# Four graph attention layers on one core: the order in which the lists of sources are made

## The chip, the cores and the metric

The kernel runs on one core of one Trainium2 chip. The metric is the device time of one execution in microseconds (us). The engines are named as in the profile: PE (TensorE, matrix products), DVE (VectorE), ACT (ScalarE), POOL (GpSimd) and SP (SyncE, which only issues transfers here).

## The reference

Four layers of graph attention over the same graph of 4096 nodes, with 256 features each. Every layer normalises `x`, projects it, weighs the sources of each target by a softmax over its neighbours and adds the result to `x`. The layers differ in their weights, in heads (1, 1, 4, 1 with a positive and a negative attention) and in the last function. Layer 0, cut to what matters:

```python
h = jnp.maximum(_layernorm(x, axis=-1), 0.0) @ W.T + b_W
e = (h @ a1)[:, None] + (h @ a2)[None, :] + b_a[0]
e = jnp.where(e > 0, e, 0.2 * e)
scores = jnp.where(adj > 0, e, -9e15)
x = x + jax.nn.softmax(scores, axis=1) @ h
```

The graph is sparse and uneven: an entry of `adj` is 1 with a probability proportional to `((1 + i) * (1 + j)) ** -0.5`, so the first nodes have many neighbours and the last ones few.

## The kernel before

The 4096 targets are 32 tiles of 128, and 4 tiles make a block of 512 (blocks 0 to 7). Sources come in the same 32 tiles; the first four of them (`DP`) are always taken whole.

**Dense and listed.** In layer 0, blocks 0 to 3 (tiles 0 to 15) are computed dense: for each of the 32 source tiles DVE makes weights of 128 x 512 (L1154) and PE multiplies them with the features in four products of 128 x 257 (L1196). This is a dense step. Blocks 4 to 7 (tiles 16 to 31) are computed from lists: for each target tile only the sources that one of its targets reads are gathered, by indirect DMAs. A listed tile has 4 steps with the first source tiles, then 1 to 5 steps with gathered rows `s_gg`, then 1 or 2 steps ("quads", `s_gq`, L1110, L1133) in which each quarter of 32 targets has rows of its own. `DENSE = (4, 2, 1, 1)`: in layer 1 only blocks 0 and 1 are dense, in layers 2 and 3 only block 0. So the lists of blocks 4 to 7 are read by all layers, those of blocks 2 and 3 from layer 1 on, and that of block 1 from layer 2 on.

**Masks.** `mask_chunk` turns the integer matrix (`s_raw`, loaded by SP, L1449) into bytes (`s_m`, L1468), stores them and notes in `seen` which sources have any edge (L1475). The masks of dense blocks are made as those blocks are computed; those of blocks 4 to 7 are made on the side, one chunk every three dense steps (`sides`). The last chunk of a block (`c == NCH - 1`) starts its list. In dense steps counted from 0, this happens at step 23 for block 4, 47 for 5, 60 for 1, 71 for 6, 92 for 2, 95 for 7 and 124 for 3.

**Lists.** `list_sources(ib, ...)` makes the lists of the four tiles of a block. It is a generator of some fifty small pieces: DVE operations on 128 x 112 or 128 x 448 (L886 to L935), prefix sums on PE (`pre`, `tot`, L868 and L870, twice), and then for each of the four tiles 28 small matmuls (`idx_ps`, L971) with one-hot matrices that DVE makes (`first`, L946), and the copy to `idx_T` (L981). Its temporary tiles exist once, so two lists overlap little.

**The gathers.** `gather` (L529) issues one indirect DMA of 128 rows from POOL, with a pause (a memset, L538) after every second one. POOL's instructions run in the order in which the program issues them. For a tile there are gathers of mask bytes (`mlist`) and of features (`s_gg`, `s_gq`), and both need `idx_T`.

**Order of the work.** `run` goes over a plan of steps, with fetch, begin, weigh and multiply 0, 2, 3 and 6 steps apart (`LEAD`). After each step it adds the step's cost to a clock of its own and takes two pieces of the first generator of the queue `lists_q`, if that is due (a piece can ask for a delay of up to 4 units). The queue is first in, first out. When a step fetches a tile whose list is not there, `listed_sources` takes pieces at once until it is:

```python
while T not in index:
    pump(lists_q, 1, force=True)
```

Listed steps of layer 0 are mixed with dense steps from dense step 48 on (`LISTED0`), one or two after each. At the end of layer 0's plan the rest of `lists_q` is taken by force; layer 1's plan comes after it. On PE, DVE, ACT and SP a scheduler sets the final order from this order of issue; POOL's order is kept.

Of the kernel before, what the change touches and what calls it, by code (L numbers as in the profile page):

```python
# [480 lines left out]
TW = tuple(FRONT[l] + GW[l] + MW * ((l, True) in MASKS_IN.values()) for l in range(4))  # L481
LEAD = (0, 2, 3, 6)
RUN = 2


@with_exitstack
def list_layers(ctx: ExitStack, tc: tile.TileContext, a: dict, out: bass.AP, flag):
# [39 lines left out]
    def gather(dst, src, index_ap, offset):  # L527
# [8 lines left out]
        gathers[0] += 1  # L536
        if gathers[0] % RUN == 0:
            nc.gpsimd.memset(pause, 0.0)  # L538
# [22 lines left out]
    def mask_rows(b, jt):  # L561
        if b not in MASKS_IN:
            return table_rows(mask_t[b], jt)
        l, behind = MASKS_IN[b]
        c0 = FRONT[l] + GW[l] if behind else 0
        return table_rows(table[l], jt)[:, :, c0 : c0 + MW].bitcast(U8)
# [116 lines left out]
    posts, lists_q = [], []  # L683
    clock = [0.0]

    def push(queue, work, delay=0.0):
        queue.append([work, clock[0] + delay])
# [703 lines left out]
    with ExitStack() as phase:  # L1391
        prep = phase.enter_context(tc.tile_pool(name="s_prep", bufs=1))
        lists_p = phase.enter_context(tc.tile_pool(name="s_lists", bufs=1))
# [41 lines left out]
            order += [(DENSE[0] + k // NCH, k % NCH) for k, at in enumerate(sides) if at == s]  # L1435
        loaded = {}
        seen = {}

        def load():

            n = len(loaded)
            if n == len(order):
                return
            ib, c = order[n]
            loaded[order[n]] = []
            for h in range(2):
                raw = stage.tile([P, half, IB], I32, name=f"s_raw_{ib}_{c}_{h}", tag="raw")
                r0 = (c * CH + h * half) * P
                nc.sync.dma_start(  # L1449
                    raw,  # L1450
                    a["adjT"][r0 : r0 + half * P, ib * IB : (ib + 1) * IB].rearrange(
                        "(c p) i -> p c i", p=P
                    ),
                )
                loaded[ib, c].append(raw)

        def mask_chunk(ib, c):

            load()
            if ib == 0:  # L1460
                behind(c)
            m = (
                mpre[:, :, ib * IB : (ib + 1) * IB]
                if c == 0
                else mpool.tile([P, CH, IB], U8, name=f"s_m_{ib}_{c}", tag="m")
            )
            for h, raw in enumerate(loaded[ib, c]):
                nc.vector.tensor_scalar(m[:, h * half : (h + 1) * half, :], raw, 0.0, None, op0=ALU.is_gt)  # L1468
            if c > 0 or ib in MASKS_IN:
                nc.sync.dma_start(mask_rows(ib, c * CH), m)  # L1470
            if ib > 0:
                if c == 0:
                    seen[ib] = lists_p.tile([P, IT * GR, JT], BF16, name=f"seen_{ib}", tag="seen", bufs=4)
                else:
                    nc.vector.tensor_reduce(  # L1475
                        seen[ib][:, :, (c - 1) * CH : c * CH].rearrange("p a j -> p j a"),
                        m.rearrange("p j i -> p (j i)")
                        .bitcast(I32)
                        .rearrange("p (j a w) -> p j a w", j=CH, w=GP // 4),
                        AX.X,  # L1480
                        ALU.max,
                    )
                if c == NCH - 1:
                    push(lists_q, list_sources(ib, seen[ib], lists_p, consts))
            return m

        def behind(c):

            if c + 4 < NIB:
                load_x(c + 4)  # L1490
            if c == 4:
                zero_rows()
            if c == 5:
                L1 = weights(1, const, prep, nc.sync)
                L1.pre = keep.tile([P, DP, GW[1]], F32, name="pre1")
                L1.rows = rows_of(L1, rows)
                L1.pool = rows
                next(L1.making)
                push(posts, L1.making, 15.0)

        def block(ib):
            masks = {}

            def get(jt):
                if jt % CH == 0:
                    masks[jt // CH] = mask_chunk(ib, jt // CH)
                for k, at in enumerate(sides):
                    if at == ib * NT + jt:
                        mask_chunk(DENSE[0] + k // NCH, k % NCH)
                ensure(lambda: L0.ready[jt])  # L1510
                return [0], [L0.g[:, jt, :]], masks[jt // CH][:, jt % CH, :]

            return Unit(L0, ib * IT, IT, NT, get, big="growb", rates=(2, 2, 1))
# [5 lines left out]
        consts = list_constants(lists_p)  # L1519
# [130 lines left out]
def gat_layers(tc: tile.TileContext, a: dict, out: bass.AP):  # L1650
    nc = tc.nc
    with tc.tile_pool(name="flag", bufs=1) as pool:
        flag = pool.tile([1, 1], I32, name="flag")

        with tc.manual_schedule(engines={mybir.EngineType.Pool}):
            list_layers(tc, a, out, flag)
        again = nc.values_load(flag[0:1, 0:1], min_val=0, max_val=1)
        with tc.If(again > 0):
            dense_layers(tc, a, out)
# [45 lines left out]
```

## Time and profile before

| | |
|---|---|
| median of 3 runs | 1554.24 us (1552.2 to 1558.08) |
| profiled execution | 1687.46 us, span 1685.7 us |
| mean granted TensorE clock in it | 0.923 |
| PE, PE weight loads | 1452.5 us (86%), 1091.1 us (65%) |
| DVE, ACT, POOL | 1176.8 us (70%), 494.3 us (29%), 1066.3 us (63%) |
| layer 0, from the span's start | to about 561 us |

The profiled execution is longer than the median of the runs and ran at a lower TensorE clock. Busy time is time in which an engine executes; the idle time before an instruction is shown with what released it. For a POOL gather the busy time is that of issuing it. Lines L... are those of the kernel before.

### The profile page before, as it was taken

The numbers are of one execution on the slowest core, as the hardware profiler recorded it, in microseconds if no ns is written. First come the engines' busy times: TensorE is split into PE (matmuls) and PEld (weight loads), VectorE is DVE, ScalarE is ACT, GpSimd is POOL, SyncE is SP. The second block draws the span as 40 slices with busy tenths as digits, with TensorE's granted clock in tenths as the row PEclk, the third lists the DMA queues.
The fourth block names the chain that finished last, engine by engine and source line by source line (L and its number), as shares of the span: only waits on it lengthen the run. The fifth ranks groups of instructions, "written<-read, shape, count | busy, mean of one in ns | idle before, by whom it ended". The sixth has DMA issues, their size and how long they took to land.

```text
span 1685.7 us, 30113 instructions
## 1 busy us (share of the span) xinstructions
PE 1452.5 (86%) x10558; PEld 1091.1 (65%) x10558; DVE 1176.8 (70%) x3383; ACT 494.3 (29%) x1558; POOL 1066.3 (63%) x1292
## 2 busy tenths in 40 slices
PE   6999899768648989988798889898877989899995
PEld 4887677557536867766545555556655767677773
DVE  6888989857727456855498889787754455577754
ACT  5631021002001112423334555466744111111111
POOL 9816888582381467757607678665665266777775
PEclk9999999979778899999999999998977999999997
DMA  7899877745322445545513344333343366767665
GB/s 264 291 325 294 280 239 248 246 125 134 87 49 87 124 118 141 146 134 146 154 51 111 92 110 110 93 108 88 104 116 100 116 181 191 220 186 216 199 183 148
DMA packets 150091, 267.82 MB, mean 159 GB/s; under 512 B 21824, under 2 KB 74637, under 8 KB 149933
## 3 DMA queue, kind: packets, MB, share of 16 engines
q0 software_dynamic: 43440, 123.46, 27.1%
q1 hardware_dynamic: 105656, 141.83, 26.2%
q8 instruction: 86, 1.41, 0.3%
q14 instruction: 73, 0.59, 0.1%
q10 hardware_dynamic: 836, 0.53, 0.1%
HBM read 224.84 MB, written 40.90 MB: 158 GB/s over the span
## 4 chain that ended last, share of the span: by engine, by line
PE 62%; DVE 16%; issue 6%; another core or an unknown queue 5%; DMA 4%; POOL 3%; ACT 2%; SPq 0%; POOLq 0%; DVEq 0%; ACTq 0%
PE s_acc L1196 36%; PE s_pj L774 8%; DVE s_p L1154 6%; PE s_acch L1213 5%; PE s_accm L1231 3%; PE s_acc L1133 3%; PE idx_ps L971 2%; PE s_sT L1039 2%; PE s_tp L742 2%; DMA s_gg<-table,idx 2%; DVE s_m L1468 1%; DMA s_gq<-table,idx 1%; DVE s_p L1163 1%; DMA s_raw<-in_adjT 1%
## 5 line engine op out<-in xcount | busy, mean ns | idle before, releaser
L529 POOL DMA_INDIRECT s_gq<-table,idx x416 | 444.0, 1067 | 183.2 <-issue 80.5
L529 POOL DMA_INDIRECT s_gg<-table,idx x265 | 291.4, 1100 | 277.7 <-issue 75.7
L1196 PE MATMUL s_acc<-g,s_p 128*128 128x257 f32 x1152 | 298.5, 405 | 22.1 <-DVE s_p L1154 17.2
L1196 PEld LDWEIGHTS s_acc<-g,s_p 128*128 128x128 f32 x1152 | 224.7, 203 | 74.4 <-DVE s_p L1154 22.4
L1196 PE MATMUL s_acc<-s_gs,s_p 128*128 128x257 f32 x896 | 212.6, 388 | 0.9 <-DVE s_p L1154 0.9
L1154 DVE SCALAR_TENSOR_TENSOR s_p<-s_grow,pre,mpre 128x128 f32<-128x128 f32 (+1 forms) x576 | 188.1, 365 | 29.3 <-PE s_acc L1196 19.6
L1196 PE MATMUL s_acc<-pre,s_p 128*128 128x257 f32 x768 | 192.6, 400 | 11.1 <-DVE s_rz L1319 3.7
L529 POOL DMA_INDIRECT mlist<-mask_t,idx x100 | 113.3, 1133 | 135.4 <-DVE idx L981 97.5
L774 PE MATMUL s_pj<-s_w,s_hT 128*128 128x259 f32 (+3 forms) x640 | 183.5, 426 | 16.0 <-ACT s_hT L744 7.5
L1154 DVE SCALAR_TENSOR_TENSOR s_p<-s_grow,s_gs,s_ms 128x512 f32<-128x512 f32 x224 | 158.5, 745 | 50.9 <-PE s_acc L1196 17.9
L1196 PEld LDWEIGHTS s_acc<-s_gs,s_p 128*128 128x128 f32 x896 | 166.8, 192 | 39.0 <-DVE s_p L1154 6.8
L1196 PEld LDWEIGHTS s_acc<-pre,s_p 128*128 128x128 f32 x768 | 150.8, 201 | 39.5 <-remote 7.5
L1196 PE MATMUL s_acc<-s_gg,s_p 128*128 128x257 f32 x530 | 139.4, 395 | 22.9 <-issue 9.3
L774 PEld LDWEIGHTS s_pj<-s_w,s_hT 128*128 128x128 f32 x640 | 125.0, 206 | 47.7 <-ACT s_hT L744 11.8
L1154 DVE SCALAR_TENSOR_TENSOR s_p<-s_grow,s_gg,mlist 128x128 f32<-128x128 f32 x370 | 119.1, 343 | 47.7 <-PE s_acc L1196 21.5
L1045 ACT ACTIVATE s_grow<-s_sT 128x256 f32<-128x256 f32 (+2 forms) x136 | 47.0, 369 | 319.0 <-PE s_sT L1039 202.6
L538 POOL MEMSET pause<- 128x256 f32 x390 | 134.5, 345 | 0.1
L1196 PEld LDWEIGHTS s_acc<-s_gg,s_p 128*128 128x128 f32 x530 | 101.2, 196 | 41.6 <-issue 17.1
L1110 DVE TENSOR_TENSOR s_p<-s_grow,s_gq 128x128 f32<-128x128 f32 (+1 forms) x168 | 52.0, 336 | 89.6 <-DMA s_gq<-table,idx 51.0
L1093 ACT ACTIVATE s_p<-s_grow,s_minus,pre 128x128 f32<-128x128 f32 x224 | 96.0, 486 | 57.9 <-PE s_accm L1231 19.2
L1213 PE MATMUL s_acch<-pre,s_p 128*64 128x65 f32 x1792 | 92.8, 238 | 23.1 <-issue 21.5
L1213 PEld LDWEIGHTS s_acch<-pre,s_p 128*64 128x64 f32 x1792 | 72.3, 145 | 61.1 <-issue 37.0
(154 smaller groups left out, 2038.2 us busy)
## 6 DMA issues: line engine op xcount, KB each, us to landing
s_raw<-in_adjT SPq DMA_DIRECT2D x128, 512.0 KB
s_gs<-table SPq DMA_DIRECT2D x28, 516.0 KB
mask_t<-s_m SPq DMA_DIRECT2D x35, 256.0 KB
table<-s_g SPq DMA_DIRECT2D x28, 258.0 KB
s_ms<-mask_t SPq DMA_DIRECT2D x28, 256.0 KB
s_gq<-table,idx POOLq DMA_INDIRECT x416
table<-s_m SPq DMA_DIRECT2D x21, 256.0 KB
s_gg<-table,idx POOLq DMA_INDIRECT x265
```

The lines of the kernel that those rows point to most:

```text
L529: nc.gpsimd.indirect_dma_start(out=dst, out_offset=None, in_=src, in_offset=bass.IndirectOffsetOnAxis(ap=index_ap, axis=0), element_offset ...
L538: nc.gpsimd.memset(pause, 0.0)
L742: nc.tensor.transpose(tp[:, c, :], zs[k][:, c * P : (c + 1) * P], ident)
L774: nc.tensor.matmul(ps, lhsT=hT[:, c, :], rhs=L.w[:, c, k * (D + 6) : k * (D + 6) + cols], start=(c == 0), stop=(c == 1),)
L1045: nc.scalar.activation(grow[:, h1:h2, :], ps[:, h1 - h0 : h2 - h0].rearrange("p h a b -> p h (a b)"), AF.Exp, scale=scale,)
L1093: nc.scalar.activation(w[:, h, :], u.grow[:, h, :], AF.Relu, scale=g[h][:, n - 1 : n], bias=minus)
L1110: nc.vector.tensor_tensor(p4[:, h0:h1], grow[:, h0:h1], c[:, h0:h1].to_broadcast([P, h1 - h0, GR, GP]), op=op)
L1133: nc.tensor.matmul(acc, lhsT=p[:, h, part], rhs=g[:, k, h * n : (h + 1) * n - 1], start=False, stop=last, skip_group_check=True,)
L1154: nc.vector.scalar_tensor_tensor(p[:, k, :], u.grow[:, h, :], g[k][:, n - 1 : n], m, op0=ALU.min if L.l == 3 and h == 1 else ALU.max, op1= ...
L1196: nc.tensor.matmul(u.accs[it][h], lhsT=p[:, k, it * P : (it + 1) * P], rhs=g[k][:, 0:n], start=first, stop=last, skip_group_check=u.quads > 0,
L1213: nc.tensor.matmul(u.accs[0][c : c + P // 2, h, :], lhsT=p[:, h, c : c + P // 2], rhs=g[h][:, 0 : DH + 1], start=first and h == 0, stop=la ...
L1231: nc.tensor.matmul(u.accs[h], lhsT=g[k][:, 0 : DH + 1], rhs=p[:, k, :], start=first, stop=last, skip_group_check=True,)
```

## The change

The lists of sources are no longer put into the queue when their block's masks are complete, but in a fixed order of blocks, `TURNS = (4, 5, 6, 1, 7, 2, 3)`. A list whose block is complete before its turn is kept in `waiting`, and it goes into the queue as soon as all blocks before it in `TURNS` are there too. Against the order before (4, 5, 1, 6, 2, 7, 3), blocks 1 and 6 change places, and blocks 2 and 7.

```diff
 RUN = 2
+TURNS = (4, 5, 6, 1, 7, 2, 3)
...
         seen = {}
+        waiting, turns = {}, list(TURNS)
...
                 if c == NCH - 1:
-                    push(lists_q, list_sources(ib, seen[ib], lists_p, consts))
+                    waiting[ib] = list_sources(ib, seen[ib], lists_p, consts)
+                    while turns and turns[0] in waiting:
+                        push(lists_q, waiting.pop(turns.pop(0)))
```

## The prediction

> **What bounds the kernel now.** I read the page's engine shares first: PE 86%, DVE 70%, POOL 63%. No single engine explains the span, so I looked for a stage in which all of them wait, and took the sums over stretches of time. These are five stretches of the second half of layer 0 and all that follows it (busy us, mean granted TensorE clock, DMA share, GB/s):
>
> ```profile
> core 0: us, PE busy (x) PEld busy (x) DVE busy (x) ACT busy (x) POOL busy (x), PEclk, DMA share, GB/s
> ...
> 325.40:396.00 70.60, 45.78 (x243) 36.28 (x242) 39.56 (x108) 9.07 (x31) 57.64 (x72) 0.79 0.55 147
> 396.00:448.20 52.20, 40.91 (x301) 34.84 (x300) 44.77 (x110) 5.77 (x22) 0.03 (x1) 0.89 0.41 114
> 448.20:515.00 66.80, 41.02 (x208) 30.62 (x207) 25.16 (x60) 4.87 (x17) 53.20 (x69) 0.67 0.25 55
> 515.00:561.00 46.00, 41.05 (x264) 33.01 (x262) 30.40 (x94) 11.37 (x44) 0.00 (x1) 0.85 0.27 84
> 561.00:1686.00 1125.00, 992.64 (x7957) 720.49 (x7955) 757.00 (x2335) 373.64 (x1120) 723.88 (x871) 0.94 0.48 137
> ```
>
> POOL, which issues every gather, does nothing from 396 to 448, then works without pause to 515, and in that last stretch PE and DVE are the ones that idle, with DMA at a quarter. So work reaches POOL late, and then everybody waits for POOL. The timeline of POOL says for what:
>
> ```profile
> 310.58 0.74 POOL L538 MEMSET pause<- 128x256 f32 x1
> 325.39 1.81 POOL L529 DMA_INDIRECT mlist<-mask_t,idx  x1 [14.07 <-DVE s_p L1154]
> ...
> 395.26 0.33 POOL L538 MEMSET pause<- 128x256 f32 x1
> 448.18 1.55 POOL L529 DMA_INDIRECT mlist<-mask_t,idx  x1 [52.59 <-DVE idx L981]
> ...
> 514.46 0.33 POOL L538 MEMSET pause<- 128x256 f32 x1
> 561.00 0.95 POOL L529 DMA_INDIRECT s_gg<-table,idx  x1 [46.21 <-DVE flag L1023]
> ```
>
> Counting gathers from tile 16 on, the one at 325 is the first of tile 24 (block 6), the one at 448 the first of tile 28 (block 7), the one at 561 the first of layer 1. The first wait is labelled with L1154, but what tile 24 needs is its list, idx_24; the second is idx_28. The DVE timeline has that list at
>
> ```profile
> 447.75 0.16 DVE L981 TENSOR_SCALAR idx<-idx_ps 128x6 int32<-128x6 f32 x1
> ...
> 561.16 0.17 DVE L981 TENSOR_SCALAR idx<-idx_ps 128x7 int32<-128x7 f32 x1 [0.81 <-PE idx_ps L971]
> ```
>
> and the second line is the last list of all (tile 15), after which layer 1's first gather goes. Between the waits POOL takes 70.2 us for tiles 24 to 27 and 66.6 us for 28 to 31, about 17 us a tile.
>
> Why idx_28 is so late follows from the code's own clock (each step adds its cost, 1.7 dense or 0.45 listed; two pieces of list work a step). Lists go in the order in which masks are complete: 4, 5, 1, 6, 2, 7, 3. When tile 24 is fetched, list 6 lacks 7 pieces; when tile 28 is fetched, list 2 is unfinished and list 7 not begun, so 29 pieces are forced at once. They run from 430 to 448 as a chain of DVE and PE with nothing beside it; until 430 PE is itself held by lists 1 and 2, which nobody reads in layer 0.
>
> **What the Trainium skill says.** TensorE: Matmul & The Clock Gate (Architectural detail: the array is 16× 32×32) says that ACT and DVE are strict first-in-first-out and GPSIMD too: one waiting gather holds all behind it. The trace agrees (52.59 us of nothing on POOL). The same page (What's actually happening) says that an idle array drops to a lower clock; here the granted clock is 0.67 in the starved stretch and 0.89 in the one before. Perfetto Trace Analysis (DMA Instruction — SWDGE) says that a POOL DMA's slice ends with its descriptors, not with the data; agreed: a gather slice is about 0.95 us, and at 338.88 PE still waits for s_gg data after 6.09 us.
>
> **The change, part by part.** No instruction is added or taken away: seven lists as before, each some 36 DVE operations (18.6 us, of which eight one-hots of 1.08) and four blocks of 28 small matmuls (about 1.9 us of PE a block; 4.6 us from one idx to the next when interleaved, 416 to 430). The gathers, their pauses (about 0.35 us per two) and the DMA transfers keep their number. From the first step of layer 1 on, the compiled order of every engine is the same. SP keeps its order but for a dozen neighbours that swap (mask and table stores against raw loads): 0, hidden by a DMA share of 0.25 to 0.55, at worst one raw load of some 5 us. TURNS makes the order 4, 5, 6, 1, 7, 2, 3. Its price is a wait: list 5 ends at clock 119 and block 6's mask is complete only at 131, so the list queue is empty for 12 units. That is filled by dense and listed steps on PE and DVE: 0.
>
> *Gain 1, tile 24.* List 6 now ends at clock 169 (idx_24 at 159, tile 24 is fetched at 180): no forced pieces. In the compiled PE order idx_24 moves from dense step 25–26 of block 2 to step 14–16. POOL's 14.07 us wait goes, and its 70 us for tiles 24 to 27 start at 311.
>
> *Gain 2, tile 28.* List 7 starts at 207, before list 2, and 8 pieces are forced instead of 29. In the PE order idx_28 stays at dense step 13 of block 3, where PE arrives at 430 now. Before that point four index blocks fewer stand in PE's stream (list 2's, minus a few small ones): between 8 us (4 x 1.9) and 18 us (4 x 4.6); I take 10. And PE's waits in 325–396, 24.5 us in all (6.09 + 6.49 + 6.41 + 5.48), are those of a POOL 14 us late; I take 14 off. So PE arrives near 430 - 24 = 406, and idx_28 follows after one block, about 410, in place of 447.8: **38 us** earlier (ends: 14, if PE arrives at 430 as now; 50, if all of PE's waits go). POOL has finished tile 27 at about 381, so it still waits some 29 us: late next is idx_28 again, not the buffers. Then 66 us of gathers, ending near 476 in place of 514.5.
>
> *Loss 1.* List 2's pieces now lie in the last third: two and a half index blocks (tiles 8 to 10) ahead of the last dense step, which stood in no one's way before. 2.5 x 2.6 = **7 us** (0 if POOL's gaps hide them, 12 at 4.6).
>
> *Loss 2.* The end. Before, list 3 alone is left when the plan ends (38 forced pieces), and its first half runs beside dense steps; from the last dense step (536.0) to layer 1 (561.0) are 25 us. Now 56 pieces are forced: list 2's last block and a half (6 us), then all of list 3, whose way from its first matmul to its first index block was 14.4 us (530.1 to 544.5), nearer 10 with DVE free, then four blocks at 4 us. About 36 us against 25: **11 us** (ends 5 and 20). It is exposed: layer 1's matmuls and gathers stand behind it.
>
> Sum: 38 - 7 - 11 = 20 us. Against the profiled execution 1687.46 gives 1667. That execution is 133 us above the median of the runs shown and had a clock of 0.923; what I move are waits on POOL and on a DVE–PE chain, so I carry the 20 us over whole: **1534 us**. A warmer clock in the starved stretch (0.67) is not counted.
>
> **Rivals.**
> *More.* POOL's wait for idx_28 shrinks towards nothing (PE at step 13 by 396), the clock stays up, and loss 1 hides in POOL's gaps: 50 - 11 = 39 us, 1515. For it: PE's busy time in 311–561 is 181 of 250 us at a mean clock of 0.80. Against: lists still cost PE and DVE what they cost.
> *Nothing.* The forced pieces only change place: 36 in the middle become 8, 38 at the end become 56, and the 38 us come out nearer 20 with 20 paid at the end: 1554. For it: total list work is the same. Against: the middle also idles POOL, which the end doesn't.
> *Slower.* One mechanism: lists 2 and 3 stand in front of layer 1 with nothing to hide them. If PE still reaches step 13 at 430, the gain is 14; two and a half blocks at 4.6 (12) and 20 at the end make 32: 18 us slower, 1572. It decides once idx_28 comes later than 448 minus the two losses, about 430 for my values. Against: the 14.07 us of tile 24 go in any case.
> *Not what it says.* TURNS could hold lists back for nothing if block 6 or 7 were complete late. The clock answers it: 12 units of empty queue for list 6, none for 7. It is inside Gain 1.
>
> **Chances.** A measurement of this kernel can tell 0.5%, 7.8 us, from no change. Forecast (10 to 32 us off) 0.69, more 0.13, nothing 0.11, slower 0.07. Faster: 0.69 + 0.13 = 0.82. The range 1514 to 1552 takes in the forecast, most of "more" and half of "nothing".
>
> **What would show it.** POOL's wait before tile 24 gone and the one before tile 28 near 29 us; idx_28 at 405 to 415; POOL's last layer 0 gather near 476; last dense step to layer 1 near 36 us in place of 25; layer 1's first gather near 541; after it 1125 us as now. I am wrong if idx_28 is not before 430, or if the end takes over 45 us.

## The result, and the profile after

The changed kernel takes 1547.08 us (median of 20 runs) against 1554.14 for the kernel before (20 runs): a ratio of 0.9955, 95% interval 0.9939 to 0.9970, or 7.1 us. The forecast was 20 us; the sign was right, the size was not. The prediction took 7.8 us as the least that can be told from no change, and the gain lies just below that.

One thing is needed to read the numbers: the kernel before takes about 1550 us in some sets of runs and 1670 to 1730 us in others, the other kernels move with it, and the profile that the prediction is built on (1687.46) is of the slower kind, while its timed runs are of the faster. So the profile after (1545.95 us, clock 0.951) is set beside a new profile of the kernel before at its level, *before_b* (1551.98 us, clock 0.943). From here on "at 1550" and "at 1690" name the two levels. In the lines shown, the changed kernel's line numbers are one higher than those of before.

Sums over stretches, first of before_b, then of the changed kernel. The stretches are: tiles 24 to 27 on POOL, its wait for tile 28's list, tiles 28 to 31, the end of layer 0, layers 1 to 3 (us, busy time of PE, PEld, DVE, ACT and POOL with the number of instructions, granted clock, DMA share, GB/s):

```profile
323.90:397.30 73.40, 62.37 (x356) 49.31 (x355) 54.64 (x147) 14.20 (x51) 62.29 (x72) 0.88 0.62 173
397.30:432.00 34.70, 22.45 (x188) 19.04 (x188) 29.82 (x71) 0.50 (x2) 0.04 (x1) 0.83 0.36 104
432.00:496.20 64.20, 55.03 (x283) 43.05 (x283) 30.67 (x75) 6.99 (x25) 53.52 (x69) 0.80 0.29 65
496.20:529.60 33.40, 26.86 (x189) 21.13 (x188) 24.44 (x79) 9.31 (x36) 0.04 (x1) 0.80 0.31 100
529.60:1550.20 1020.60, 940.35 (x7957) 691.14 (x7955) 755.34 (x2335) 375.43 (x1120) 733.82 (x871) 0.96 0.54 151
```

```profile
310.00:389.10 79.10, 69.68 (x409) 55.29 (x408) 69.23 (x183) 14.59 (x53) 67.81 (x74) 0.98 0.70 203
389.10:408.90 19.80, 15.49 (x95) 12.43 (x94) 14.55 (x44) 0.50 (x2) 0.00 (x0) 0.95 0.51 128
408.90:478.50 69.60, 56.44 (x297) 44.66 (x296) 43.37 (x111) 6.99 (x25) 58.95 (x69) 0.82 0.35 79
478.50:522.60 44.10, 36.16 (x305) 29.15 (x305) 32.17 (x90) 10.00 (x36) 4.76 (x4) 0.81 0.27 82
522.60:1544.10 1021.50, 936.63 (x7957) 689.42 (x7956) 755.52 (x2335) 375.37 (x1120) 732.84 (x867) 0.96 0.54 151
```

The last lines answer where the expected gain is not: layers 1 to 3 take 1020.6 and 1021.5 us. Nothing was given back there. All of the 7 us, and all that is missing, lies in layer 0. The second and the fourth lines show the trade: POOL's wait in the middle is 34.7 and 19.8 us long, the end 33.4 and 44.1. POOL's timeline has the turning points, in before_b and in the changed kernel:

```profile
323.91 1.81 POOL L529 DMA_INDIRECT mlist<-mask_t,idx  x1 [14.08 <-DVE s_p L1154]
...
432.03 1.55 POOL L529 DMA_INDIRECT mlist<-mask_t,idx  x1 [34.69 <-DVE idx L981]
...
529.67 0.95 POOL L529 DMA_INDIRECT s_gg<-table,idx  x1 [33.43 <-DVE flag L1023]
```

```profile
408.91 1.81 POOL L530 DMA_INDIRECT mlist<-mask_t,idx  x1 [19.85 <-DVE idx L982]
...
517.31 1.81 POOL L530 DMA_INDIRECT s_gg<-table,idx  x1 [38.81 <-DVE first L947]
```

The wait before tile 24 (14.08) is gone, tile 28 starts at 408.91 in place of 432.03. Read together with PE's timeline, the 7 us come out as a sum of three terms (us from the span's start; the last dense step is step 31 of block 3, taken in its middle):

| | before_b | after | gain so far |
|---|---|---|---|
| PE starts dense step 13 of block 3 | 412.9 | 405.8 | 7.1 |
| POOL starts tile 28 | 432.0 | 408.9 | 23.1 |
| last dense step on PE | 502.1 | 490.4 | 11.7 |
| layer 1's first targets on PE | 529.6 | 522.6 | 7.0 |

So the middle gains 23.1, the dense steps then lose 11.4 of it (23.1 - 11.7), and the end 4.7 more (27.5 us from the last dense step to layer 1, now 32.2). That is 7.0, the measured difference.

The 23.1 are mostly the forced chain. PE's rows of it in before_b (the row at 411.48 ends with the first product of dense step 13, from 412.86; then list 7's prefix sums and tile 28's index block), and the same work in the changed kernel, where step 13 starts at 405.77:

```profile
411.48 1.98 PE L1196 MATMUL s_acc<-g,s_p 128*128 128x257 f32 x8
...
414.11 0.36 PE L868 MATMUL pre_p<-pure,s_tri 128*128 128x448 f16 x1
...
423.14 0.21 PE L868 MATMUL pre_s<-shared,s_tri 128*128 128x112 f16 x1 [4.58 <-DVE shared L914]
...
429.60 1.80 PE L971 MATMUL idx_ps<-val,first 128*128 128x6 f16 x28 [6.19 <-DVE val L935]
```

```profile
397.38 0.23 PE L869 MATMUL pre_s<-shared,s_tri 128*128 128x112 f16 x1 [2.61 <-DVE shared L915]
...
404.95 0.96 PE L972 MATMUL idx_ps<-val,first 128*128 128x6 f16 x14 [1.69 <-DVE val L936]
405.77 1.89 PE L1197 MATMUL s_acc<-g,s_p 128*128 128x257 f32 x6
407.46 0.98 PE L972 MATMUL idx_ps<-val,first 128*128 128x6 f16 x14
```

Before, PE arrives at step 13 at 412.9 and POOL goes at 432.0, 19.2 us later, with PE waiting 4.58 and 6.19 us for DVE inside. Now the prefix sums and half of the index block stand ahead of that step, with waits of 2.61 and 1.69 us, and POOL goes 3.1 us after PE's arrival. That is 16.0 us; PE's own earlier arrival is only 7.1.

### The profile page after: what moved, and what is told of

It reads as the page before. It is cut to its first block, busy times and chain, and to the rows that moved or that the text cites. A ratio compares the mean times of both kernels' runs of the same rounds, so it can differ in the third digit from the quotient of the medians.

```text
span 1544.1 us, 30112 instructions
## 1 busy us (share of the span) xinstructions
PE 1390.0 (90%) x10558; PEld 1056.1 (68%) x10558; DVE 1174.4 (76%) x3383; ACT 496.6 (32%) x1558; POOL 1095.9 (71%) x1292
## 4 chain that ended last, share of the span: by engine, by line
PE 56%; DVE 18%; POOL 12%; DMA 8%; issue 4%; ACT 2%; POOLq 0%; DVEq 0%; SPq 0%; ACTq 0%
PE s_acc L1197 34%; PE s_pj L775 8%; DVE s_p L1155 7%; DMA s_gq<-table,idx 5%; POOL s_gq L530 5%; PE s_acch L1214 3%; PE s_acc L1134 3%; PE s_accm L1232 3%; POOL mlist L530 2%; POOL s_gg L530 2%; DVE s_p L1164 2%; PE idx_ps L972 2%; POOL pause L539 1%; PE s_sT L1040 1%; PE s_tp L743 1%
## 5 line engine op out<-in xcount | busy, mean ns | idle before, releaser
L530 POOL DMA_INDIRECT s_gq<-table,idx x416 | 463.2, 1113 | 127.1 <-issue 80.7
L530 POOL DMA_INDIRECT s_gg<-table,idx x265 | 299.9, 1132 | 208.8 <-issue 66.9
L1197 PE MATMUL s_acc<-pre,s_p 128*128 128x257 f32 x768 | 183.8, 387 | 1.5 <-DVE s_p L1155 1.5
L1197 PEld LDWEIGHTS s_acc<-pre,s_p 128*128 128x128 f32 x768 | 145.6, 194 | 25.2 <-DVE s_p L1155 2.1
L1197 PE MATMUL s_acc<-s_gg,s_p 128*128 128x257 f32 x530 | 132.7, 384 | 2.3 <-DVE s_p L1155 2.3
L1232 PE MATMUL s_accm<-s_p,s_gs 128*65 128x512 f32 x224 | 100.9, 600 | 0.9 <-DVE s_p L1155 0.9
L1470 DVE TENSOR_SCALAR s_m<-s_raw 128x1024 uint8<-128x1024 int32 x112 | 80.3, 730 | 10.0 <-DMA s_raw<-in_adjT 10.0
```

What stands on the lines that cost most here:

```text
L530: nc.gpsimd.indirect_dma_start(out=dst, out_offset=None, in_=src, in_offset=bass.IndirectOffsetOnAxis(ap=index_ap, axis=0), element_offset ...
L1197: nc.tensor.matmul(u.accs[it][h], lhsT=p[:, k, it * P : (it + 1) * P], rhs=g[k][:, 0:n], start=first, stop=last, skip_group_check=u.quads > 0,
L1232: nc.tensor.matmul(u.accs[h], lhsT=g[k][:, 0 : DH + 1], rhs=p[:, k, :], start=first, stop=last, skip_group_check=True,)
```

## The experiments

Theory: the gain is the earlier list of tile 28, less list work moved behind it; its size depends on the level at which the program runs, and layers 1 to 3 have no part in it. Rivals: the gain was 20 us and layers 1 to 3 took it back; or the exchange of blocks 1 and 6 is what costs; or it was never the order but the pace at which list work is taken. The runs are three sets, where the kernel before took 1701.78 (43 runs), 1552.14 (16) and 1686.13 us (7). Each set is on another chip, so a level can't be told apart from a chip here. Ratios are to the kernel before in the same set.

**The kernel before again.** No edit. In the first set *before_again*, in the second *before_b*.

> The kernel before, unchanged, for a profile that can be laid beside the one of the changed kernel (span 1544.1 us, layer 0 to 522.6, the rest 1021.5 us). Theory A, my sum was made against a stretched execution: layer 0 ends near 530 us here in place of 561, POOL's wait for the list of tile 28 is there but shorter (20 to 45 us in place of 52.6), and the rest takes 1020 to 1025 us. Theory B, layer 0 did gain about 20 us or more and a later layer gave it back: layer 0 ends at 542 or later and the rest takes 1012 us or less.

Measured: 1696.34 us, span 1694.6, clock 0.922. POOL waits 51.92 us before tile 28, as in the first profile (52.59). At this level it decides neither theory.

> The kernel before, unchanged, once more for its profile, since the first repeat took 1696 us and cannot be laid beside the 1544.1 us of the changed kernel. At the level of 1554 us: Theory A expects layer 0 to end near 530 us with a wait for the list of tile 28 of 20 to 45 us, and 1020 to 1025 us after it. Theory B expects layer 0 to end at 542 us or later, and a rest of 1012 us or less. At the level of 1700 us it says again what the first repeat said: layer 0 to 561 to 578 us, a wait of 52 us, 1117 to 1125 us after it.

Measured: 1551.98 us, the tables above. Layer 0 ends at 529.6, the wait is 34.69 and the rest takes 1020.6 us: theory A. The two profiles of before differ in what ends DVE's waits. The waits of DVE from 300 to 560, first at 1690 (the profile that the prediction used), then at 1550 (releaser, us in total, times, longest):

```profile
DVE den L1256 <- remote: 24.0, 3, 9.0
DVE s_p L1154 <- remote: 17.5, 5, 8.2
...
DVE s_p L1154 <- DMA s_gg<-table,idx: 6.4, 1, 6.4
```

```profile
DVE s_p L1154 <- PE s_acc L1196: 18.9, 17, 3.0
DVE s_p L1110 <- DMA s_gq<-table,idx: 18.2, 7, 5.4
DVE s_p L1154 <- DMA s_gg<-table,idx: 16.8, 6, 6.2
```

"Remote" means that nothing in this core's records ended the wait. In the first trace 41.5 us of DVE from 300 to 560 go that way, in pauses of up to 9 us. In the second no engine has such a wait of 1 us or more in the whole span, and so it is in all five traces at 1550; each of the nine at 1690 has them, 58 to 208 us over all engines. What makes the pauses isn't settled here.

**The changed kernel again.** No edit. *change_b* in the second set, *change_c* in the third.

> The changed kernel, unchanged, in the same call as the others. Theory A: what the change gains depends on the level. At 1700 us it gains 20 us or more (ratio 0.988 or lower), as my sum had it against a profile at that level; at 1554 us about 7 us (ratio 0.9955). Theory B: the ratio is near 0.9955 at both.

Measured: 1546.39 us (12 runs), ratio 0.9960 (0.9935 to 0.9985). POOL starts tile 28 at 410.54 after a wait of 19.46, layer 1's first gather is at 517.85. The 7 us repeat.

> The changed kernel once more, beside the others. If before takes about 1552 us in this call: 0.9955 again, within 0.003. If it takes about 1700 us: theory 'level' says that the gain is 20 us or more there (ratio 0.982 to 0.989), as the two halves of the change measured at that level; the rival says 7 us at either (0.996).

Measured: 1654.05 us, ratio 0.9844 (0.9756 to 0.9932): 26 us faster, somewhere from 12 to 41, on a chip where before takes 1686. POOL there:

```profile
419.42 1.81 POOL L530 DMA_INDIRECT mlist<-mask_t,idx  x1 [29.52 <-DVE idx L982]
...
529.85 1.73 POOL L530 DMA_INDIRECT s_gg<-table,idx  x1 [39.79 <-DVE first L947]
```

and the sums of its last two stretches (the end of layer 0, layers 1 to 3), columns as above:

```profile
490.10:535.10 45.00, 37.83 (x319) 30.12 (x317) 32.53 (x91) 10.01 (x36) 4.68 (x4) 0.79 0.26 80
535.10:1656.40 1121.30, 988.61 (x7957) 718.52 (x7955) 757.67 (x2335) 373.84 (x1120) 718.93 (x867) 0.94 0.49 138
```

Layers 1 to 3 take 1121.3 us, against 1125.0 in the first profile of before: again no part of the difference. Layer 1 starts at 535.1 here and at 561.0 there, 25.9 us earlier. The same code is worth 7 us at one level and some 26 at the other; the two intervals don't meet, though narrowly (0.9932 and 0.9939), and the larger figure rests on one set with four runs of the changed kernel.

**Half of the change: blocks 1 and 6 alone.** *swap16*, first set.

```diff
-TURNS = (4, 5, 6, 1, 7, 2, 3)
+TURNS = (4, 5, 6, 1, 2, 7, 3)
```

> TURNS = (4, 5, 6, 1, 2, 7, 3): of the two exchanges only that of blocks 1 and 6. By the code's clock 50 pieces are forced at tile 28 (29 before, 8 with both exchanges) and 38 at the end, as before. If the gain comes from tile 28's list, this gains nothing or loses: 1550 to 1562 us. If it comes from tile 24's wait, about 1547 us as with the whole change.

Measured: 1695.43 us, ratio 0.9948 (0.9917 to 0.9978). The wait before tile 24 is gone, but by the code's clock 50 pieces are now forced at tile 28 (29 before), and POOL waits 57.92 us there. Taking away the first wait lengthens the next one: POOL comes earlier to a list that is not ready. Still, the ratio is a gain of some 9 us, where the theory of tile 28's list said none or a loss; what brings it isn't shown, and this half alone wasn't run at 1550.

**The other half: blocks 2 and 7 alone.** *swap27* in the first set, *swap27_b* in the second.

```diff
-TURNS = (4, 5, 6, 1, 7, 2, 3)
+TURNS = (4, 5, 1, 6, 7, 2, 3)
```

> TURNS = (4, 5, 1, 6, 7, 2, 3): only the exchange of blocks 2 and 7. Tile 24 forces 7 pieces as before, tile 28 none, 42 pieces are left at the end (38 before, 56 with both). If tile 28's list is what counts, it gains as much as the whole change or more, 1538 to 1547 us, because the end is shorter by 14 pieces. If tile 24's wait counts, it stays near 1554 us.

Measured: 1683.38 us (median of 22 runs). They scatter from 1648.72 to 1709.5, and the ratio on record, 0.978 (0.973 to 0.983), rests on the lowest four. The means of all runs of both kernels give 0.988 (0.985 to 0.992 by resampling the runs), some 20 us.

> TURNS = (4, 5, 1, 6, 7, 2, 3), only the exchange of blocks 2 and 7, beside the whole change on one chip. 42 forced pieces are left at the end, 56 with the whole change; tile 24 forces 7 again. If the end counts for more than tile 24's wait, it is faster than the whole change by 3 to 8 us; if tile 24's 14 us count, slower by 3 to 8 us.

Measured: 1539.21 us, ratio 0.9915 (0.9890 to 0.9941). POOL's waits in this run, as totals by releaser:

```profile
POOL s_gg L530 <- DVE flag L1024: 42.2, 1, 42.2
...
POOL mlist L530 <- DVE s_p L1155: 14.1, 1, 14.1
...
POOL mlist L530 <- DVE idx L982: 5.6, 1, 5.6
```

The wait before tile 24 stays (14.1) and the one before tile 28 is down to 5.6 us. So this half alone does more at 1550 than the whole change: 13 us against 6 to 7. Added to it, the exchange of 1 and 6 costs 7 us there (1546.39 against 1539.21 in one set). Most of it is at the end: the last dense step is at 489.8 here and at 490.4 in the changed kernel, but layer 1 follows 28.1 us later in place of 32.2. Whether this half gains more at 1690 isn't shown: over all runs 0.988 (0.985 to 0.992) there and 0.9915 (0.989 to 0.994) here overlap.

**All that layer 0 reads first.** *needfirst* in the first set, *needfirst_b* in the third.

```diff
-TURNS = (4, 5, 6, 1, 7, 2, 3)
+TURNS = (4, 5, 6, 7, 1, 2, 3)
```

> TURNS = (4, 5, 6, 7, 1, 2, 3): all lists of layer 0 first. Neither tile 24 nor tile 28 forces any piece, POOL should never wait for a list, but 84 pieces are left at the end (38 before, 56 with the change). If the forced pieces at the end cost their whole length there (about 0.6 us each, 28 more than with the change), it is slower than the change by 10 to 20 us, near 1560 us, in spite of POOL's wait gone. If POOL's waits are the larger part, it is faster than the change: 1535 to 1543 us.

Measured: 1671.27 us, ratio 0.9826 (0.9785 to 0.9866). POOL still waits 20.80 us before tile 28, where the expectation had no wait for a list; the whole change wasn't run in this set.

> Order 4, 5, 6, 7, 1, 2, 3 at two pieces a step: both lists that layer 0 reads come first, nothing is forced in the middle, 84 pieces at the end. The three terms read from the changed kernel (tile 28's list, the dense steps delayed, the end) say: POOL waits 13 to 18 us before tile 28 (19.9 in the changed kernel), the end is some 5 us longer, so the same as the changed kernel within 4 us: 0.993 to 0.998 of before if before takes about 1552 us. If before takes about 1700 us here, 0.983 as measured in the first batch. A rival, that every us of POOL's wait in the middle comes out at the end of the run, says 5 to 7 us faster than the changed kernel.

Measured: 1653.86 us, ratio 0.9823 (0.9716 to 0.993), not to be told from the whole change in that set (1654.05) with four runs of each. No piece is forced in the middle and POOL waits 10.00 us before tile 28; but 84 pieces are forced at the end, and POOL waits 45.65 us before layer 1 and 38.3 us soon after, where the kernel before has 14.8. What the middle gains beyond the change, the end takes: the last dense step is at 483.1 against 503.3 in change_c, layer 1 on PE at 534.4 against 535.1.

**The pace.** If forced pieces are the cost, more pieces a step should be worth more than any order. *rate3_27* (second set) has the order of swap27 and three pieces after a step of layer 0 in place of two:

```diff
-            return Unit(L0, ib * IT, IT, NT, get, big="growb", rates=(2, 2, 1))
+            return Unit(L0, ib * IT, IT, NT, get, big="growb", rates=(2, 3, 1))
...
-                rates=(1, 2, 0),
+                rates=(1, 3, 0),
```

> TURNS = (4, 5, 1, 6, 7, 2, 3) and three pieces of list work after each step of layer 0 instead of two. By the code's clock the lists of tiles 24 and 28 are then there when they are fetched (0 forced pieces for each), and 34 are left at the end, fewer than before (38). If forced pieces are what costs, in the middle and at the end alike, this beats the whole change by 10 to 20 us. If list work costs the same wherever it stands, it is within 4 us of the order without the higher rate.

Measured: 1515.24 us, ratio 0.9768 (0.9726 to 0.9811), better than both kernels: 2.3% under the one before, and 31 us under the changed one where 10 to 20 were expected. The largest totals of POOL's waits from 300 to 600 have no list in them any more (the 38.7 us are those before layer 1):

```profile
POOL s_gg L530 <- DMA s_w<-in_L_gnn_W: 38.7, 1, 38.7
POOL s_gq L530 <- issue: 15.0, 64, 0.3
POOL s_gg L530 <- PE s_acc L1197: 14.4, 5, 13.6
```

PE starts layer 1 at 493.9 in place of 529.6, and layers 1 to 3 take what they took (1017.9 us): so an order and a pace that leave nothing forced in the middle and less at the end start layer 1 about 36 us earlier, of which the change as it stands collects 7. Against swap27_b in the same set, which differs only in the pace, it is 24 us.

*rate3_before* and *rate3_change* (third set) are the same two edits on the kernel before and on the changed kernel.

> The order of the kernel before (lists start when their masks are complete: 4, 5, 1, 6, 2, 7, 3), but three pieces of list work after a step of layer 0 instead of two. By the code's clock 12 pieces are forced at tile 28 instead of 29, and 34 at the end instead of 38. Theory 'rate': the forced chain ahead of tile 28 is what cost, whatever list is ahead; the gain of the 1515 us version is then mostly here, 22 to 30 us (ratio near 0.983), with POOL's wait before tile 28 down from 34.7 to under 15 us. Theory 'order': list 2 still stands ahead of list 7, so the wait stays near 25 us and the gain is 8 to 12 us (ratio near 0.994).

Measured: 1639.71 us, ratio 0.9764 (0.9663 to 0.9865). The time is that of "rate"; the wait isn't. POOL still waits 32.92 us before tile 28, and the wait before tile 24 is what went. So the mechanism expected was only half seen, and with no profile of before in that set the place of the gain isn't shown.

> The changed kernel's order (4, 5, 6, 1, 7, 2, 3) with three pieces of list work after a step. 0 pieces forced at tile 28, 38 at the end (56 in the changed kernel). Theory: with the rate raised, list 7 is ready in time and the end is as short as in the kernel before, so 28 to 38 us faster than before (ratio near 0.978), the same as with only blocks 2 and 7 exchanged. Rival: bringing list 6 ahead of list 1 still sends list work behind the last dense step, 10 us less gain (ratio near 0.985).

Measured: 1637.1 us, ratio 0.974 (0.9661 to 0.9819). The size is that of the theory. But POOL waits 26.95 us before tile 28 here and 48.5 before layer 1. The two versions with the higher pace can't be told apart (0.9764 and 0.974), so at 1690 the order adds nothing that four runs of each could show. At 1550 the pace was tried only with the order 4, 5, 1, 6, 7, 2, 3.

## Why the prediction was off

The sign, the mechanism and the places were right; the size was not. The term that failed is PE's arrival at dense step 13, forecast 24 us earlier and measured 7.1. Behind it stands "I carry the 20 us over whole", with the reason that the waits moved are those "on POOL and on a DVE–PE chain". They were, but in the profile used PE came to that chain 16 us later than in before_b, and most of that lies in waits that before_b doesn't have.

**Gain 1 (tile 24)** is right: no wait before tile 24 in any run of the changed kernel.

**Gain 2 (tile 28), 38 us forecast, 23.1 measured.** The place was right: idx_28 forecast at 410, on DVE at 408.5. The place that it left was not 447.8 but 431.6. The mis-sized term is "I take 14 off" and "I take 10", 24 us in all: PE's arrival moved by 7.1. How much of that is the 10, four index blocks fewer with 8 as the low end, wasn't measured apart. The 14 came from adding up PE's four waits from 325 to 396 and calling them all those of a late POOL. PE's waits in that stretch, in that profile and then in before_b:

```profile
PE s_acc L1196 <- DVE s_p L1154: 6.5, 1, 6.5
PE pre_p L868 <- issue: 6.4, 1, 6.4
PE s_acc L1196 <- DMA s_gg<-table,idx: 6.1, 1, 6.1
PE s_tp L742 <- DVE s_z L728: 5.5, 1, 5.5
```

```profile
PE s_acc L1196 <- DVE s_p L1154: 6.6, 2, 5.9
PE s_pj L774 <- DVE off_p L873: 3.7, 1, 3.7
```

Only one of the four, 6.1 us, waits for gathered rows. One has no releaser, and the two on DVE follow DVE's own pauses without a releaser (8.31 us before L1256 at 358, 6.67 at 390). In before_b that stretch has two waits of over 3 us, 5.87 and 3.70, and PE starts dense step 13 at 412.9 with no change made, against 428.8 in the profile used. What the prediction took off as a gain was for the most part the difference between the levels. The other part of this term was right: the chain from the prefix sums to the index copy, 17.8 us in the profile used (430.0 to 447.75), is 17.5 in before_b (414.11 to 431.61), and the "one block", 4, after it is 2.7 from PE's arrival to the copy.

**POOL's wait before tile 28, 29 us forecast, 19.85 measured.** POOL ended tile 27 at 389, not 381: its 74 instructions of that stretch took 67.81 us, 916 ns each, against 801 (57.64 us for 72) in the profile used and 865 in before_b.

**Loss 1, 7 us forecast, 11.4 measured**, inside the bound of 12. About 6 are what was forecast, list 2's blocks behind the last gathers: from POOL's last gather to the last dense step PE needs 11.9 us (478.5 to 490.4), before 5.9 (496.2 to 502.1). The other 5.4 were not foreseen: POOL takes 69.6 us for tiles 28 to 31 instead of 64.2, with the same 69 instructions.

**Loss 2, 11 us forecast, 4.7 measured**, just under its lower end of 5. From the last dense step to layer 1 "about 36 us against 25" are 32.2 against 27.5. The prediction's own parts make 36 only with 14.4 us for list 3's way; with the "nearer 10" that it prefers, 6 + 10 + 16 are 32. That this is the measured total is luck: the parts are 7.4 for the rest of list 2, 4.9 before list 3's first matmul, which no part had, 11.3 for its way and 8.7 for its four blocks, half of the 16. A small slip beside it: the last list's copy (561.16) comes after layer 1's first gather (561.00), not before it; no sum rests on that.

**The sum.** 23.1 - 11.4 - 4.7 = 7.0 in place of 38 - 7 - 11 = 20. Read at 1690, against the profile that was used, the same terms are: tile 28 at 419.4 in place of 448.2 (28.8), the last dense step at 503.3 in place of 536.0 (32.7, so nothing is lost on the way), 31.8 against 25.0 at the end (6.8), net 25.9. That is nearer to the forecast than the 7. These are two executions of different sets, and before_again starts layer 1 at 577.5 rather than 561.0, so the start of layer 1 alone is loose by some 16 us. PE's arrival at step 13 is too: 416.6 in change_c is 12 us before the profile used (428.8) and 24 before before_again (440.4), so whether the 24 held at that level stays open. Only the ratio of change_c carries the size. Its 26 us (12 to 41) hold the 20.

**The rivals.** "Nothing" (20 us gained, 20 paid) had the right shape: 23 gained, 16 paid. "Slower" asked for idx_28 later than 430 and failed on that; "more" needed POOL's wait to vanish, which the change doesn't do and rate3_27 does. The prediction's own test for being wrong (idx_28 not before 430, or an end of over 45 us) didn't catch it, since it tested the places after and not the place before.

## What to carry over

Before a saving is worked out from a profiled execution, set its own time and clock beside the timed runs; if they differ as here by over 8%, the waits in it are not those of the runs, and a wait whose releaser the profile doesn't show shouldn't be credited to the engine that one means to speed up. Where a queue is served at a fixed pace and the rest is taken by force, reordering mostly moves the forced part from one place to another (here 23 us gained, 16 paid); raising the pace can remove it (rate3_27, 24 us beyond the order alone). A change in two parts is worth trying by halves: here one half gained 13 us and both together 6 to 7. Follow each wait that goes to the next one: without tile 24's, tile 28's grew (swap16, 57.9 us).

## What the hardware showed

Not expected: POOL's gathers take longer to issue in stretches where DVE has more to do. Groups of POOL for tiles 28 to 31, in before_b (DVE busy 48% of the stretch) and in the changed kernel (62%), with the same instructions:

```profile
L529 POOL DMA_INDIRECT mlist<-mask_t,idx x23 | 23.6, 1026 | 40.0 <-DVE idx L981 34.7 <-issue 5.1 <-DVE s_p L1154 0.2
L529 POOL DMA_INDIRECT s_gq<-table,idx x16 | 15.8, 990 | 3.8 <-issue 3.8
```

```profile
L530 POOL DMA_INDIRECT mlist<-mask_t,idx x23 | 26.3, 1144 | 25.2 <-DVE idx L982 19.8 <-issue 5.0 <-DVE s_mv L721 0.2
L530 POOL DMA_INDIRECT s_gq<-table,idx x16 | 17.6, 1102 | 3.8 <-issue 3.4 <-PE s_sT L1040 0.3
```

1026 ns become 1144, and 990 become 1102. Over the stretches of the first profile, of before_b and of the changed kernel the mean of a POOL instruction rises with DVE's share: 771 ns at 38%, 776 at 48%, 801 at 56%, 854 at 62%, 865 at 74%, 916 at 88%. The two stretches of change_c, at 61% and 72%, both have 870, so the relation is loose. The Trainium skill (SBUF — State Buffer, SBUF: two separate sides) says that DVE in some of its modes locks GpSimd out of a port pair that they share, so that the descriptors of a POOL DMA are not written meanwhile. The numbers go in that direction, but no trace here tells in which mode DVE's instructions ran, and no run separated this from other causes, the DMA load among them.

The second is the two levels themselves, in before_b and in the first profile: the same instructions, 1550.2 us and 1685.7 us of span, PE busy 1398.8 and 1452.5, and pauses of 5 us and more on DVE, ACT and PE at the slower one (up to 9.0, 11.8 and 7.7 us) that no record of the core explains. Some 31 us of the difference lie in layer 0 (layer 1 starts at 529.6 and 561.0), the other 104 in layers 1 to 3 (1020.6 and 1125.0).
